# The head of a one-core kernel in written order: tokens loaded in pairs, other engines for copies and type tables, maxima in four row blocks, constants behind the scores

## The chip, the core and the metric

The kernel runs on one core of a Trainium2 chip. The core's engines each work through their own list of instructions: TensorE (PE; its weight loads are listed as PEld), VectorE (DVE), ScalarE (ACT), GpSimd (POOL) and SyncE (SP), which here only issues transfers. They wait for one another through semaphores. Data lies in device memory, in SBUF (128 partitions) or, for matmul results, in PSUM. The metric is the device time of one execution in microseconds (us); lower is better.

## What is computed

Two layers work on `x` of 8 sequences, 256 tokens, 128 features, all in float32. Only the first step of the first layer is touched by the change:

```python
attn_in = jnp.tanh(jnp.einsum('bsd,da->bsa', hidden, W1) + b1)     # A = 32
scores = jnp.einsum('bsa,a->bs', attn_in, v)
prefix_m = l <= j;  postfix_m = l >= j;  cloze_m = l != j
mask = where(pt == 0, prefix_m, where(pt == 1, postfix_m, cloze_m))  # pt: one type per sequence
p = softmax(where(mask, scores[:, None, :], NEG_INF), axis=-1)
pooled = einsum('bjl,bld->bjd', p, hidden) / cnt
...
logits = einsum('bld,ed->ble', pooled, gate_weight)
kth_val = sort(logits.reshape(-1))[expert_k - 1]
gates = logits * (logits >= kth_val)
h = gelu(einsum('bld,ehd->bleh', pooled, w1) + b1)                   # 8 experts, 512 hidden
x = x + sum over experts of gates * (h @ w2 + b2)
```

The second layer adapts each sequence by its language (two small matrices, a layer norm), takes the two best of eight experts for each token, runs those experts and adds the result to `x`.

## The kernel before

The work falls into three stages. The **head** (lines 90 to 345) loads `x`, scores the tokens and pools them. The **first layer** (`layer`, L801 and L781) runs all eight experts on all 2048 tokens, five units of 512 or 256 tokens; beside it generators (`poolings`, `threshold`, `adapt`) are advanced a step at a time by `pump`. The **second layer** fetches tiles of 128 sorted rows and runs one expert on each (L857, L866), then adds up and stores.

The head in the order of its data. There are four groups `g`, each of two sequences, so 512 tokens. `xg[g]` holds the tokens, two on each partition and sequence, in rows of `XW` = 137: 128 features, 8 gate products, and a one. SP and ACT each load half of every group (L105). TensorE turns the tokens (`xTp`, L227); the copy to `xT` goes to ScalarE for groups 0 and 2 (L232) and to VectorE for 1 and 3 (L230). `products` multiplies by `W1` and the gate columns (`xa`, L206), VectorE adds `b1` (L209), ScalarE takes the tanh (L210) and copies the gate products into `xg` (L211). `scores` multiplies by `v` and sums (L214, L215) into `sl`, one column for 128 tokens. `bv` holds `b1` and `v` on all partitions, made by a matmul of `diag` and `ones` (`bvp`, L234, L236).

The softmax needs for each query the largest score that it may see. `sl` is turned to rows, one per sequence (`scp`, L251), two scans run along them, forwards and backwards (L254, L256), and two operations make of them and of `out8` (what a sequence's type rules out) the maxima, 8 rows (L258, L259). A matmul with one column of `ident`, broadcast, copies a row to all 128 partitions: `tops` (L265). `probs` subtracts them from a table of masks, chosen by the sequence's type (`hide`, `kind`, L274), and ScalarE takes the exponential with the score as bias (L277). `pool` multiplies by the tokens (`poolp`, L287), `scaled` divides by the sum and by `cnt` (L294 to L298), and `turned` turns the result for the first layer (`poolTp`, L304; `poolT`, L306).

Small tables come from the types `ptb`: `e0`, `e1`, `kind`, `out8`, on VectorE (L135 to L152). GpSimd issues the loads of `col`, `bva` and `ptb`, builds `ident` and `hide`, and then the constants of later stages: `nhalf`, `rank`, `tri`, `dest`, `kth`, `empty`, `steps`, `nowhere`, `used` (L349 to L509). `used` is first read by a copy of eight columns on VectorE (L705), which belongs to the second layer's lists. `pass_time` (L193) is a filler: matmuls into a PSUM tile that nobody reads.

The order in each engine's list is set by a scheduler from the program, except where a block is marked as manual (`manual_schedule`), which keeps it as written. Before, only the end of the kernel is so marked.

Of the kernel before, what the change touches and what calls it, by code (L numbers as in the profile page):

```python
# [10 lines left out]
F32 = mybir.dt.float32  # L11
I32 = mybir.dt.int32
AF = mybir.ActivationFunctionType
# [58 lines left out]
def tile_adaln_ffn_d2(ctx: ExitStack, tc: tile.TileContext, x, ptype, lang, cols, b1v,  # L72
# [17 lines left out]
    xg = []  # L90
    for g in range(NG):

        xg.append(keep.tile([P, GT, XW], F32, tag="xg", name=f"xg{g}"))
    ptb = const.tile([P, B], I32, name="ptb")
# [3 lines left out]
    ident = const.tile([P, P], F32, name="ident")  # L98
    make_identity(nc, ident)
    nc.gpsimd.dma_start(out=col, in_=cols)  # L100
    nc.gpsimd.dma_start(out=bva, in_=b1v)
    nc.gpsimd.dma_start(out=ptb, in_=ptype.partition_broadcast(P))
    for g in range(NG):
        for i, queue in enumerate((nc.sync, nc.scalar)):
            queue.dma_start(out=xg[g][:, 2 * i:2 * i + 2, :D], in_=xv[g, i])  # L105
    nc.sync.dma_start(out=lgi, in_=lang.partition_broadcast(P))

# [12 lines left out]
    ones = const.tile([P, P], F32, name="ones")  # L120
    nc.vector.memset(ones, 1.0)
# [4 lines left out]
    for i, (sign, keeps) in enumerate(((-1, ALU.is_ge), (1, ALU.is_ge), (1, ALU.not_equal))):  # L126
        nc.gpsimd.affine_select(out=hide[:, i, :], in_=hide[:, i, :],
                                pattern=[[sign, 2], [-sign, 2], [-2 * sign, P]], compare_op=keeps, fill=NEG,
                                base=0, channel_multiplier=2 * sign)
    jrow = const.tile([P, 2], F32, name="jrow")  # L130
# [4 lines left out]
    nc.vector.tensor_copy(ptf, ptb)  # L135
    e0 = const.tile([P, B], F32, name="e0")
    nc.vector.tensor_scalar(e0, ptf, 0.0, None, ALU.is_equal)
    e1 = const.tile([P, B], F32, name="e1")
    nc.vector.tensor_scalar(e1, ptf, 1.0, None, ALU.is_equal)
    kind = const.tile([P, B], I32, name="kind")  # L140
    with nc.allow_low_precision("0, 1 or 2"):
        nc.vector.scalar_tensor_tensor(kind, e0, 2.0, e1, ALU.mult, ALU.add)
        nc.vector.tensor_scalar(kind, kind, -1, 2, ALU.mult, ALU.add)


    out8 = const.tile([B, 3], F32, name="out8")
    for i, flag in enumerate((e0, e1)):
        own = small.tile([B, B], F32, tag="own", name=f"own{i}", bufs=2)
        nc.vector.scalar_tensor_tensor(own, flag[:B, :], NEG, ident[:B, :B], ALU.mult, ALU.mult)
        nc.vector.tensor_reduce(out8[:, i:i + 1], own, AX.X, ALU.add)  # L150
    nc.vector.tensor_tensor(out8[:, 2:3], out8[:, 0:1], out8[:, 1:2], ALU.add)
    nc.vector.tensor_scalar(out8[:, 2:3], out8[:, 2:3], -1.0, NEG, ALU.mult, ALU.add)  # L152
# [30 lines left out]
    fwd, bwd, rows = fwd[:B, :], bwd[:B, :], top[:B, :]  # L183
    nc.gpsimd.memset(fwd[:, 0:1], NEG)
    nc.gpsimd.memset(bwd[:, S - 1:], NEG)
    nc.gpsimd.memset(top, 0.0)

# [7 lines left out]
    pass_time(5, ident, ident)  # L195


    sl = small.tile([P, NT], F32, tag="sl", name="sl", bufs=1)
    xas = {}

    def products(g):

        space = (psy, "y") if g < 2 else (psb, "big")
        xa = space[0].tile([P, GT, A + E], F32, tag=space[1], name=f"xa{g}")
        for t in range(GT):
            nc.tensor.matmul(xa[:, t, :], lhsT=xT[g][:, t * P:(t + 1) * P], rhs=col[:, C_W1:C_W1 + A + E],  # L206
                             start=True, stop=True)
        pass_time(1, ident, xT[g][:, :S])
        nc.vector.tensor_tensor(at[:, g], xa[:, :, :A], bv[:, 0].unsqueeze(1).to_broadcast([P, GT, A]), ALU.add)  # L209
        nc.scalar.activation(at[:, g], at[:, g], AF.Tanh)  # L210
        nc.scalar.copy(xg[g][:, :, D:D + E], xa[:, :, A:])  # L211

    def scores(g):
        nc.vector.tensor_tensor(at[:, g], at[:, g], bv[:, 1].unsqueeze(1).to_broadcast([P, GT, A]), ALU.mult)  # L214
        nc.vector.tensor_reduce(sl[:, g * GT:(g + 1) * GT], at[:, g], AX.X, ALU.add)  # L215
# [5 lines left out]
    bvp = psy.tile([P, 2, A], F32, tag="y", name="bvp")  # L221
    bv = const.tile([P, 2, A], F32, name="bv")

    for g in range(NG):
        tp = psb.tile([P, GT, P], F32, tag="big", name=f"xTp{g}")
        for t in range(GT):
            nc.tensor.transpose(tp[:, t, :], xg[g][:, t, :D], ident)  # L227
        xT[g] = keep.tile([P, GN], F32, tag="xT", name=f"xT{g}")
        if g % 2:
            nc.vector.tensor_copy(xT[g], tp.rearrange("p t d -> p (t d)"))  # L230
        else:
            nc.scalar.copy(xT[g], tp.rearrange("p t d -> p (t d)"))  # L232
        if not g:
            nc.tensor.matmul(bvp.rearrange("p c a -> p (c a)"), lhsT=ones[:A, :],  # L234
                             rhs=diag.rearrange("k c a -> k (c a)"), start=True, stop=True)
            nc.vector.tensor_copy(bv, bvp)  # L236
        else:
            products(g - 1)
        if g > 1:
            scores(g - 2)  # L240
    products(NG - 1)
    scores(NG - 2)
    scores(NG - 1)
    kinds = []
    for b in range(B):
        kinds.append(nc.values_load(kind[0:1, b:b + 1], engines=(DVE,), min_val=0, max_val=2,
                                    skip_runtime_bounds_check_because="2 - 2 e0 - e1, of flags"))

    sp = pss.tile([B, S], F32, tag="sm", name="scp")
    for u in range(2):  # L250
        nc.tensor.transpose(sp.rearrange("b (p u) -> b p u", u=2)[:, :, u],  # L251
                            sl.rearrange("p (b u) -> p b u", u=2)[:, :, u], ident)
    pass_time(5, sl[:, NT - 1:].to_broadcast([P, P]), xT[0][:, :S])
    nc.vector.tensor_tensor_scan(fwd[:, 1:], sp[:, :S - 1], out8[:, 1:2].to_broadcast([B, S - 1]), NEG,  # L254
                                 ALU.max, ALU.add)
    nc.vector.tensor_tensor_scan(bwd[:, S - 2::-1], sp[:, :0:-1], out8[:, 0:1].to_broadcast([B, S - 1]), NEG,  # L256
                                 ALU.max, ALU.add)
    nc.vector.scalar_tensor_tensor(fwd, sp, out8[:, 2:3], fwd, ALU.add, ALU.max)  # L258
    nc.vector.tensor_tensor(rows.rearrange("b (u p) -> b p u", u=2), fwd.rearrange("b (p u) -> b p u", u=2),  # L259
                            bwd.rearrange("b (p u) -> b p u", u=2), ALU.max)  # L260
    tops = []
    for g in range(NG):
        tp = psb.tile([P, 2, S], F32, tag="big", name=f"top{g}")
        for i in range(2):
            nc.tensor.matmul(tp[:, i, :], lhsT=ident[:, 2 * g + i:2 * g + i + 1].to_broadcast([P, P]), rhs=top,  # L265
                             start=True, stop=True)
        tops.append(tp)
# [3 lines left out]
    def probs(b):  # L271
        g, i = b // 2, b % 2
        m = scratch(f"probs{b}")
        nc.vector.tensor_tensor(m, hide[:, bass.ds(kinds[b], 1), :].rearrange("p k (t j) -> p (k t) j", t=2),  # L274
                                tops[g][:, i, :].unsqueeze(1).to_broadcast([P, 2, S]), ALU.subtract)
        for lt in range(2):
            nc.scalar.activation(m[:, lt, :], m[:, lt, :], AF.Exp, bias=sl[:, 2 * b + lt:2 * b + lt + 1])  # L277
# [71 lines left out]
    nc.gpsimd.memset(nhalf, -0.5)  # L349
# [46 lines left out]
    nc.gpsimd.memset(nowhere, float(NOWHERE))  # L396

# [108 lines left out]
    used = const.tile([P, E], F32, name="used")  # L506

    holding = const.tile([P, E], F32, name="holding")
    nc.gpsimd.memset(used, 0.0)  # L509
# [63 lines left out]
    def adapt(u, acc):  # L573
# [11 lines left out]
        ha = work.tile([A + 1, 2, S], F32, tag="ha", name=f"ha{u}")  # L585
        nc.gpsimd.memset(ha[A:A + 1, :, :], 1.0)  # L586
# [428 lines left out]
```

## Time and profile before

| what | value |
|---|---|
| five runs | 379.33, 382.74, 383.48, 385.68, 377.87 us |
| their median | 382.74 us |
| the profiled execution, its own time | 378.91 us |
| its span, first to last instruction | 377.1 us |
| granted TensorE clock, mean | 0.98 |
| DMA | 46.12 MB, mean 122 GB/s |
| GpSimd busy | 95.6 us, 25% of the span |

All durations are from that one profiled execution. In the profile's lists L12 is line 12 of the kernel; a group's line names the tile written and those read, their partitions and elements, and how many instructions there were; a float32 matmul shows as two instructions, a transpose as one. Busy shares of 40 equal slices are given in tenths. Idle time is put down to the event that ended it. A timeline merges neighbouring instructions of one kind into one line, with the time from the first's start to the last's end.

The waits of the first 35 us, the larger ones, in all and the longest single one:

```profile
engine line waited for: us in total, times, longest us
ACT probs L277 <- DVE probs L274: 5.4, 1, 5.4
ACT front L210 <- DVE front L209: 4.5, 4, 1.7
ACT xT L232 <- PE xTp L227: 3.8, 2, 2.6
...
DVE diag L219 <- DMA bva<-in_b1v_dram: 3.6, 1, 3.6
...
PE idle L193 <- POOL ident masks.py:199: 2.6, 1, 2.6
```

### The profile page before, as it was taken

The page shows a single profiled execution, that of the slowest core. Times are in us where ns is not written, and L with a number is a line of the kernel's source. Part 1 is how long each engine was busy: PE and PEld are TensorE (multiplying, and loading weights), DVE is VectorE, ACT ScalarE, POOL GpSimd, SP SyncE. Part 2 cuts the span into 40 slices and gives each one's busy share as a digit, 9 for nine tenths or more (in the row PEclk, how much of TensorE's full clock was granted, in tenths as well). Part 3 has the DMA queues.
Part 4 walks back from the last instruction along what each step waited for, and adds up shares of the span by engine and source line. Part 5 has one row for each costly group of instructions (what it writes and reads, how often), then busy time and mean ns, then how long its engine had stood idle before and what let it go on. Part 6 is the DMA issues. An engine that isn't in the chain of part 4 may idle for free. (4 is left out here: it accounts for less than half of the span.)

```text
span 377.1 us, 5944 instructions
## 1 busy us (share of the span) xinstructions
PE 347.6 (92%) x1596; PEld 234.9 (62%) x1596; DVE 199.5 (53%) x835; ACT 166.7 (44%) x387; POOL 95.6 (25%) x141
## 2 busy tenths in 40 slices
PE   6999999999999999999999999999979987899920
PEld 6796444444444445444544688878859886799920
DVE  4676556551334676654611465786575674234344
ACT  2265443454453224333353335435625745566730
POOL 8100000000000030452160012072043655534450
PEclk9999999999999999999999999999989999999985
DMA  7935999004224201111130001124642653567426
GB/s 208 374 75 149 365 379 364 8 0 113 91 64 132 56 30 56 56 49 35 37 83 22 28 20 45 36 79 134 181 122 84 167 173 94 164 190 195 150 91 196
DMA packets 34466, 46.12 MB, mean 122 GB/s; under 512 B 5444, under 2 KB 17622, under 8 KB 34432
## 3 DMA queue, kind: packets, MB, share of 16 engines
q1 hardware_dynamic: 29888, 39.98, 35.3%
q0 software_dynamic: 2304, 4.37, 3.4%
q10 hardware_dynamic: 2240, 1.38, 1.2%
q8 instruction: 14, 0.23, 0.2%
q14 instruction: 20, 0.16, 0.2%
HBM read 31.57 MB, written 14.39 MB: 122 GB/s over the span
## 5 line engine op out<-in xcount | busy, mean ns | idle before, releaser
L803 ACT ACTIVATE hT_first<-hp_first,col 128x512 f32<-128x512 f32 (+1 forms) x160 | 93.4, 601 | 101.4 <-PE hp_first L801 99.4
L801 PE MATMUL hp_first<-poolT,w 128*128 128x512 f32 (+1 forms) x320 | 120.6, 512 | 0.0
L781 PE MATMUL yp_first<-hT_first,w 128*128 128x512 f32 (+1 forms) x320 | 120.5, 511 | 0.0
L781 PEld LDWEIGHTS yp_first<-hT_first,w 128*128 128x128 f32 x320 | 58.9, 190 | 42.5 <-issue 38.6
L801 PEld LDWEIGHTS hp_first<-poolT,w 128*128 128x128 f32 x320 | 59.0, 190 | 42.2 <-issue 37.2
L688 POOL DMA_INDIRECT xs<-zr,pos x32 | 32.3, 1008 | 65.3 <-DVE pos L686 27.9
L859 ACT ACTIVATE hs<-hps,b 128x128 f32<-128x128 f32 x144 | 40.3, 368 | 17.2 <-PE hps L857 8.2
L872 POOL DMA_INDIRECT ys<-yt,xt x36 | 35.7, 991 | 43.4 <-ACT hs L859 26.6
L866 PE MATMUL yps<-w,hs 128*128 x288 | 40.1, 282 | 3.3 <-DVE yt L870 1.7
L857 PE MATMUL hps<-xc,wt 128*128 128x128 f32 x288 | 39.4, 279 | 1.7 <-issue 1.7
L866 PEld LDWEIGHTS yps<-w,hs 128*128 128x128 f32 x288 | 35.7, 193 | 5.3 <-ACT hs L859 2.5
L769 DVE SCALAR_TENSOR_TENSOR part_first<-yp_first,col,gbc_first 128x512 f32<-128x512 f32 (+1 forms) x28 | 17.2, 616 | 40.4 <-PE yp_first L781 40.2
L857 PEld LDWEIGHTS hps<-xc,wt 128*128 128x128 f32 x288 | 36.0, 195 | 2.4 <-issue 1.4
L871 ACT ACTIVATE yt<-yt,xt 128x128 f32<-128x128 f32 x36 | 14.6, 405 | 22.3 <-issue 10.6
L850 DVE COPY b<-col 128x4 f32 x36 | 7.1, 197 | 25.3 <-ACT hs L859 22.4
L771 DVE TENSOR_TENSOR acc_first<-acc_first,part_first 128x512 f32<-128x512 f32 (+1 forms) x35 | 20.1, 581 | 0.6
L410 POOL DMA_DIRECT2D gd_L<-gT_L x1 | 0.7, 653 | 75.3 <-DVE gT_L L408 75.3
L586 POOL MEMSET ha<- 1x512 f32 x5 | 2.6, 516 | 67.6 <-PE dp L595 67.4
L870 DVE TENSOR_TENSOR yt<-yps,b2all 128x128 f32<-128x128 f32 x36 | 10.6, 294 | 13.4 <-PE yps L866 7.6
L848 DVE TENSOR_SCALAR xc<-xtp,col 128x128 f32<-128x128 f32 x36 | 14.4, 402 | 3.7 <-PE xtp L846 2.4
L789 ACT ACTIVATE y_first<-yp_first,col 128x512 f32<-128x512 f32 x8 | 5.5, 687 | 24.2 <-PE yp_first L781 24.2
L424 DVE TENSOR_SCALAR_CACHE_REDUCE fl<-logit,tr 128x128 f32<-128x128 f32 x46 | 13.5, 343 | 0.6
(213 smaller groups left out, 316.0 us busy)
## 6 DMA issues: line engine op xcount, KB each, us to landing
wt<-in_w_dram SPq DMA_DIRECT2D x36, 256.0 KB
xs<-empty SPq DMA_DIRECT2D x1, 8580.0 KB
w<-in_w_dram SPq DMA_DIRECT2D x24, 256.0 KB
gbc_first<-gd_L SPq DMA_DIRECT2D x24, 256.0 KB
xt<-xs SPq DMA_DIRECT2D x36, 65.0 KB
gbc_first<-gd_L SPq DMA_DIRECT2D x16, 128.0 KB
yg<-ys SPq DMA_DIRECT2D x5, 256.0 KB
lgb<-in_lgb_dram SPq DMA_DIRECT2D x8, 128.0 KB
```

The costliest lines, as they stand in the source:

```text
L688: move = nc.gpsimd.indirect_dma_start(out=xs, out_offset=bass.IndirectOffsetOnAxis(ap=pos[:, t:t + 1], axis=0), in_=zr[s][:, t, :], in_off ...
L769: nc.vector.scalar_tensor_tensor(part, y, bias, gbc, ALU.add, ALU.mult)
L771: nc.vector.tensor_tensor(accs[u], accs[u], part, ALU.add)
L781: nc.tensor.matmul(yp, lhsT=w2s[e][:, c, :], rhs=hT[:, c, :], start=(c == 0), stop=(c == HC - 1))
L801: nc.tensor.matmul(hp, lhsT=w1s[e][:, c * P:(c + 1) * P], rhs=sources[g][:, o * P:o * P + n], start=True, stop=True)
L803: nc.scalar.activation(hT[:, c, :], hp, act, bias=col[:, cb1 + e * HC + c:cb1 + e * HC + c + 1])
L848: nc.vector.tensor_scalar(xc, tp, col[:, C_LG:C_LG + 1], col[:, C_LB:C_LB + 1], ALU.mult, ALU.add)
L857: nc.tensor.matmul(hp[:, c, :], lhsT=wt[:, c * P:(c + 1) * P], rhs=xc, start=True, stop=True)
L859: nc.scalar.activation(hT[:, c, :], hp[:, c, :], AF.Gelu, bias=b1[:, c:c + 1])
L866: nc.tensor.matmul(yp, lhsT=hT[:, c, :], rhs=w21[:, bass.ds(ek, 1), c * D:(c + 1) * D], start=(c == 0), stop=(c == HC - 1))
L871: nc.scalar.activation(yt, yt, AF.Copy, scale=xt[:, D + 1:D + 2])
L872: move = nc.gpsimd.indirect_dma_start(out=ys, out_offset=bass.IndirectOffsetOnAxis(ap=xt.bitcast(I32)[:, D:D + 1], axis=0), in_=yt, in_off ...
```

## The change

All lines of the head are put under a manual schedule for TensorE, VectorE, ScalarE and GpSimd (`beginning`), which ends after the constants. Within it:

- Each group's tokens are loaded twice: first into `xp`, a tile of four of the scratch ring, with the two tokens of a partition side by side, by SP and ACT; then, by SP alone and ahead of the weights, into `xg` as before. The transposes read `xp`, the pooling reads `xg`.
- `ident` is finished before GpSimd issues its loads, and `bva` is issued ahead of `col`. The first filler reads `ones` instead of `ident` and runs seven times; other fillers change in number and place.
- All four `xT` copies are ScalarE's. Transposes of groups 2 and 3 stand between the products of groups 0 to 2. The copies of the gate products come after the last tanh.
- `e0`, `e1`, `kind` are made on GpSimd. `sl` becomes 2 x 128 columns with a group's two sequences at columns 32 g and 32 g + 1, so that the turned scores, the scans and the maxima lie on 128 partitions, a group in each block of 32; `at_home` and `out8` follow that layout, and `out8` comes between the scores of groups 1 and 2.
- The `tops` matmuls read 32 rows each, first all four groups' first sequence, then their second.
- GpSimd's `nhalf`, and so all constants behind it, wait for the last score. `used` and two tiles `ha` (their row of ones was set anew in every `adapt` before) are set at the end of them.
- In the lists, VectorE's `c1` and `cnt` operations now follow the eight `probs`; they stood among earlier work before. The copy out of `used` (L705 before, L733 after) stands right ahead of the first `probs`.

The core of the diff:

```diff
+        xp.append(work.tile([P, 2, S], F32, tag="scr", name=f"xp{g}", bufs=NSCR))
...
+    beginning.enter_context(tc.manual_schedule(engines={PE, DVE, ACT, POOL}))
+    ones = const.tile([P, P], F32, name="ones")
+    nc.vector.memset(ones, 1.0)
     make_identity(nc, ident)
+    nc.gpsimd.dma_start(out=bva, in_=b1v)
     nc.gpsimd.dma_start(out=col, in_=cols)
-    nc.gpsimd.dma_start(out=bva, in_=b1v)
     nc.gpsimd.dma_start(out=ptb, in_=ptype.partition_broadcast(P))
     for g in range(NG):
         for i, queue in enumerate((nc.sync, nc.scalar)):
-            queue.dma_start(out=xg[g][:, 2 * i:2 * i + 2, :D], in_=xv[g, i])
+            queue.dma_start(out=xp[g][:, i, :], in_=xv[g, i].rearrange("p u d -> p (u d)"))
     nc.sync.dma_start(out=lgi, in_=lang.partition_broadcast(P))
+    for g in range(NG):
+        for i in range(2):
+            nc.sync.dma_start(out=xg[g][:, 2 * i:2 * i + 2, :D], in_=xv[g, i])
...
-    nc.vector.tensor_copy(ptf, ptb)
+    nc.gpsimd.tensor_copy(ptf, ptb)
...
-    nc.vector.tensor_scalar(e0, ptf, 0.0, None, ALU.is_equal)
+    nc.gpsimd.tensor_scalar(e0, ptf, 0.0, None, ALU.is_equal)
...
+    nc.gpsimd.tensor_scalar(ptf, e0, -2.0, 2.0, ALU.mult, ALU.add)
+    nc.gpsimd.tensor_tensor(ptf, ptf, e1, ALU.subtract)
+    nc.gpsimd.tensor_copy(kind, ptf)
...
-    pass_time(5, ident, ident)
+    pass_time(7, ones, ones)
...
+    turned_tokens(0)
+    pass_time(1, ones, ones)
+    turned_tokens(1)
+    nc.tensor.matmul(bvp.rearrange("p c a -> p (c a)"), lhsT=ones[:A, :],
+                     rhs=diag.rearrange("k c a -> k (c a)"), start=True, stop=True)
+    nc.vector.tensor_copy(bv, bvp)
+    products(0)
+    turned_tokens(2)
+    bent(0)
+    products(1)
+    turned_tokens(3)
+    scores(0)
+    bent(1)
+    products(2)
+    pass_time(1, ident, xT[2][:, :P])
+    scores(1)
+    bent(2)
+    out8 = const.tile([P, 3], F32, name="out8")
+    for i, flag in enumerate((e0, e1)):
+        own = small.tile([P, B], F32, tag="own", name=f"own{i}", bufs=2)
+        nc.vector.tensor_tensor(own, flag, at_home, ALU.mult)
+        nc.vector.tensor_reduce(out8[:, i:i + 1], own, AX.X, ALU.add)
...
+    products(3)
+    pass_time(2, ident, xT[3][:, :S])
+    scores(2)
+    bent(3)
+    scores(3)
+    for g in range(NG):
+        nc.scalar.copy(xg[g][:, :, D:D + E], xas[g][:, :, A:])
...
+    tops = [psb.tile([P, 2, S], F32, tag="big", name=f"top{g}") for g in range(NG)]
+    for i in range(2):
+        for g in range(NG):
+            quadrant = slice(g * A, (g + 1) * A)
+            nc.tensor.matmul(tops[g][:, i, :], lhsT=ident[quadrant, g * A + i:g * A + i + 1].to_broadcast([A, P]),
+                             rhs=top[quadrant, :], start=True, stop=True)
+    pass_time(2, ident, xT[0][:, :S])
...
-    nc.gpsimd.memset(nhalf, -0.5)
+    begin = nc.gpsimd.memset(nhalf, -0.5)
+    tc.add_manual_dep(begin.ins, scored[-1].ins.name, SYNC, reason="leaves the vector engine its port until then")
...
+    used = const.tile([P, E], F32, name="used")
+    nc.gpsimd.memset(used, 0.0)
+    has = [const.tile([A + 1, 2, S], F32, name=f"ha{i}") for i in range(2)]
+    for ha in has:
+        nc.gpsimd.memset(ha[A:A + 1, :, :], 1.0)
+    beginning.close()
...
-    nc.gpsimd.memset(used, 0.0)
...
-        ha = work.tile([A + 1, 2, S], F32, tag="ha", name=f"ha{u}")
-        nc.gpsimd.memset(ha[A:A + 1, :, :], 1.0)
+        ha = has[u % 2]
```

## The prediction

> **What bounds the kernel now.** I read the page's busy shares and slices first, then the timeline of each engine over the first 45 us, then the waits of that stretch, then the instruction lists of both programs.
>
> ```profile
> PE 347.6 (92%) x1596; PEld 234.9 (62%) x1596; DVE 199.5 (53%) x835; ACT 166.7 (44%) x387; POOL 95.6 (25%) x141
> ...
> PE   6999999999999999999999999999979987899920
> ```
>
> TensorE is busy 92% of the span, from the first slice to the tail. So the change, all of it ahead of the first expert matmul, can move the end only by moving that matmul (30.22 us) along TensorE's line; from there both programs issue the same TensorE work.
>
> ```profile
> 2.62 2.50 PE L193 MATMUL idle<-ident 128*128 128x128 f32 x10 [2.62 <-POOL ident masks.py:199]
> 4.91 1.06 PE L227 MATMUL xTp<-ident,xg 128*128 128x128 f32 x4
> 6.58 0.68 PE L234 MATMUL bvp<-diag,ones 32*128 32x64 f32 x2 [0.61 <-DVE diag L219]
> 7.20 2.82 PE L227 MATMUL xTp<-ident,xg 128*128 128x128 f32 x12
> 9.81 1.28 PE L206 MATMUL xa<-col,xT 128*128 128x40 f32 x8
> ...
> 16.48 0.39 PE L251 MATMUL scp<-ident,sl 128*8 128x128 f32 x2 [0.92 <-DVE sl L215]
> ...
> 19.39 3.69 PE L265 MATMUL top<-front,ident 128*128 128x256 f32 x16 [0.36 <-DVE front L259]
> 22.91 5.80 PE L287 MATMUL poolp<-xg,probs 128*128 128x137 f32 x48
> 28.55 0.60 PE L304 MATMUL poolTp<-ident,pooled 128*128 128x128 f32 x4
> ...
> 30.22 1.12 PE L801 MATMUL hp_first<-poolT,w 128*128 128x512 f32 x2
> ```
>
> Columns: start, length, engine, line, operation, and in brackets the idle time before and who ended it. Up to 16.48 the chain is transposes, products, scores; then 2.9 us of VectorE scans with filler on TensorE; then TensorE is full from 19.39.
>
> ```profile
> 9.27 0.20 DVE L236 COPY bv<-bvp 128x64 f32<-128x64 f32 x1
> ...
> 9.68 1.27 DVE L230 COPY xT<-xTp 128x512 f32<-128x512 f32 x2
> ...
> 16.14 0.29 DVE L215 TENSOR_REDUCE sl<-front 128x4 f32<-128x128 f32 x1
> ...
> 18.64 0.60 DVE L259 TENSOR_TENSOR front<-front 8x256 f32<-8x256 f32 x1
> ...
> 19.35 0.15 DVE L705 COPY at<-used 128x8 f32<-128x8 f32 x1
> ...
> 20.52 4.88 DVE L274 TENSOR_TENSOR probs<-hide,top 128x512 f32<-128x512 f32 x8 [0.83 <-PE top L265]
> ```
>
> VectorE's copy of xT1 waits at 9.68 behind the type tables, which wait for ptb until 7.43. The fifth line counts later: a copy out of `used`, hoisted to just ahead of the probs.
>
> Call R the end of the last score: 16.14 + 0.29 = 16.43. The first expert matmul is at R + 13.79.
>
> **Up to R.** Removed: the type tables and `out8` ahead of the xT copies on VectorE, both VectorE xT copies (now ScalarE, 0.59 each at L232), two of four 256-column fillers between products, and the start on `ident` (2.62): the filler now reads `ones`, written 0.92 to 1.09, so TensorE starts at about 1.2. Added: two fillers, one more among the transposes, a 0.2 us memset of `sl` in VectorE's idle time before 6.32. The order is now worked through by TensorE's pitches (weight loads: filler 2.21/10 = 0.22, transpose 2.42/12 = 0.20, products 1.37 the first, about 0.8 a group later):
> 7 fillers 1.2 + 14 x 0.22 = 4.3; xTp0 5.1; filler 5.55; xTp1 6.35; bvp 6.85; products 0, first of their kind, 7.95; xTp2 8.65 (0.7, between cold and warm transposes); products 1 9.45; xTp3 10.15; products 2 10.95; short filler 11.2; products 3 12.0.
> ScalarE's copies fit between. `bva` now goes ahead of `col` on POOL's queue: `bva` landed at 6.25, 3.2 us after its issue ended, `ptb` 3.75 after; `col` issued by about 3.0 lands by 6.2 to 6.8, just in time for 6.85; if 0.7 later, R moves by as much. VectorE has the last word: after add 2 (11.3) and score 1 (11.9) stand the six `out8` operations, each waiting for the one before, at 0.17 (L150 to L152) about 1.0: 12.9. Then add 3 and two scores: 15.10 to 16.43 took 1.33 before, so R = 14.2. **Gain 2.2**, between 1.5 (TensorE at the slow pace throughout, `col` late) and 3.2 (fast pace from the second transpose, short `out8`).
>
> Doubled x loads: 1 MB more on SP's queue, ahead of all 16 first-layer weights, the languages' loads, w21, b2 and the 8.6 MB `xs` fill. At 276 to 357 GB/s (DMA rates of 2 to 10 us) 2.9 to 3.8 us. Cover: the 16 weights were issued by 14.3 and the first is read at 30.22; the `xs` fill left at 38.54 and the next issue on that queue is at 88.72, the first scatter past 130. Without that cover it would cost its 3.8. Price 0. The paired loads move 1 KB runs instead of 512 B: the first transpose was not waiting for data, 0. The `ha` memsets (0.52 each) leave GpSimd's later work, where GpSimd is a quarter busy: 0.
>
> **From R on.** Scans over 128 partitions instead of 8 keep their length (255 elements a partition either way). Three things move.
>
> (1) The constants. GpSimd's `nhalf` now waits for the last score, and 21 operations queue behind it, in this order.
>
> ```profile
> 6.00 0.13 POOL L349 MEMSET nhalf<- 128x4 f32 x1
> ...
> 8.04 0.12 POOL L509 MEMSET used<- 128x8 f32 x1
> ...
> 8.80 0.24 POOL L387 CAST steps<-kth 128x3 int32<-128x3 f32 x1
> ...
> 10.22 1.26 POOL L392 TENSOR_SCALAR steps<-steps 128x3 int32<-128x3 int32 x4
> ```
>
> The last line holds four operations. `used` was the 15th and done at 8.16; now it is behind the `steps` chain too. Pitches: `nhalf` to `steps` memset 1.93, two waits for a memset ahead of its select 0.3, zr copy 0.15, cast 0.23, first product 0.25, the four 1.26, nowhere and used 0.25: 4.4, plus 0.2 for two hand-overs. So `used` lands at R + 4.6 to 4.7. VectorE's copy out of `used` (after: L733) still stands right ahead of the probs in its list, and the eight probs, their register loads and all that follows wait behind it. The scans end at R + 2.8 and the probs began at R + 4.09; now they begin at R + 4.8 plus the first register load, no longer hidden: 0.06 (free) to 0.71 (SP's gap between an lgb issue and the next lw at L164, 16.51 to 17.22), I take 0.4: **R + 5.2**. This wait replaces the one for the tops.
>
> Beside it VectorE's last max (two SBUF inputs) meets GpSimd's 0.54 us memset of `empty`. VectorE's 8-element cast at 7.43 took 0.76 and its compare 0.54 beside GpSimd, against 0.18 at L143: up to 0.6 more, hidden under R + 5.2, but added if the `used` chain slows too (bound 0 to 0.6; nearest is 0, as L143 also ran beside GpSimd). [...]
>
> (2) The tops: eight matmuls over 32 rows, four to a round, in place of eight over 128. No row shows two row blocks at once: between 8 x 0.46 = 3.7 (as L265) and 2 x 0.46 = 0.9. The first prob waits for its tile's second matmul, now the fifth: R + 2.96 + 0.3 to 2.5, at most R + 5.5. Two fillers (0.92) follow. poolp therefore starts at R + 6.6 (R + 5.2, plus 0.73 to the exp and about 0.65 for it and the hand-over) or R + 7.5; before R + 6.48. I take the short end, because a round has separate inputs, weights and PSUM tiles. [...]
>
> (3) `cnt` (eight operations, four with waits, 1.1) moves from ahead of the probs to behind them. VectorE: probs R + 5.2 to 10.1, cnt 11.2, the first two `scaled` 1.5 (25.32 to 26.64 took 1.3, interleaved): R + 12.7. poolp's six end at R + 12.4, so poolTp0 starts at R + 12.7, was R + 12.0 by its weight load; **0.7 given back** (0.3 if `used` is early, 1.3 if the tops run one by one, up to 1.9 with the collision). Behind it the other `scaled`, 4.5 of VectorE time (27.81 to 33.50, less the copy's 0.68 and a wait of 0.52), reach poolTp1 about 0.7 late as well, no more.
>
> **Sum.** 378.91 (span 377.1 and 1.8 around it) - 2.2 + 0.7 = 377.4. That profiled run is 3.8 under the median of the five, 382.74, so the forecast on the median is **381.2**.
>
> **Rivals.**
> *Faster.* `used` arrives before the tops and rounds overlap: probs at R + 4.1, VectorE ready for poolTp0 at R + 11.6, first expert matmul R + 13.3, 0.45 won instead of 0.7 lost. With R 3.2 earlier: 3.7, 379.1; with an out8 block under 0.8, past 3.8. For: TensorE's early start. Against: GpSimd's 4.4 us.
> *Slower.* TensorE's clock falls back. Its idle before poolp grows from 0 to about 1.8 us, after one of 1.2 before the scores' turn. The same shape took 421 ns (xTp) and 272 ns (poolTp), and the slow pace lasted from 2.62 to 9.8. If 7.2 us at 1.8 times the pitch return, 3.2 are lost: 381.2 + 3.2 = 384.4; after both gaps 387.6. It decides at gaps past 1.7: after an idle 1.72 at 326.43 eight matmuls took 1.21 instead of 1.06, no fallback. [...]
> *Not what it says.* `col` late and `out8` in the way hold R at 15.7: nothing won, 382.7.
>
> **Chances.** What a measurement here can tell from no change is about 1%, 3.8 us. Forecast 0.50 (within 1% but for 0.05 faster and 0.03 slower by measurement), faster 0.28 (0.23 over 1%, rest within), slower 0.14 (0.09 over 1%), nothing 0.08. Sums: faster 0.28, same 0.60, slower 0.12. Range: the fast rival 379.1 less about 1.7 for the spread of medians (five runs span 377.87 to 385.68), to the slow one's single gap: 377.4 to 384.4.
>
> **What would show it.** R near 14.2; `used` ended by GpSimd past R + 4.5 with VectorE idle ahead of L733, released by POOL; poolp matmuls still 280 ns; poolTp0 at R + 12.7; first expert matmul 1 to 2 us before 30.2. Wrong if VectorE waits for the tops instead, if xTp stays at 421 ns past 9 us, or if what is won at the first expert matmul is not found at the end.

## The result, and the profile after

The changed kernel takes 376.94 us, the median of 52 runs (374.26 to 380.46), beside 380.81 us for the kernel before in 94 runs (376.64 to 386.91). The ratio is 0.9942, with a 95% interval of 0.9925 to 0.9958: 2.2 us won, clear of no change, but less than the 1% that one takes for a difference here. (The medians are of all runs; the ratio leaves out those over 1.5% above their kernel's fastest, 36 of the 94 and 2 of the changed kernel's, so it is nearer to 1.) On the median that the forecast was made on, the ratio gives 382.74 x 0.9942 = 380.5; the forecast was 381.2, its range 377.4 to 384.4. The profiled execution took 377.3 us, its span 375.6 us; the sum had 377.4, and that this close a match is partly luck is shown further down. The busy shares and slices of the page are almost those of before:

```profile
PE 347.8 (93%) x1604; PEld 234.8 (63%) x1604; DVE 198.4 (53%) x829; ACT 168.4 (45%) x389; POOL 95.9 (26%) x145
...
PE   8889999999999999999999999999979987999920
```

TensorE does the same work, 347.8 us of it, and the whole difference is in where the first expert matmul stands.

TensorE's timeline in the head of the changed kernel; the columns are as in the prediction (start, length, engine, line, operation, idle time before it and its releaser):

```profile
1.13 3.35 PE L193 MATMUL idle<-ones 128*128 128x128 f32 x14 [1.13 <-DVE ones L104]
4.28 1.06 PE L230 MATMUL xTp<-ident,xp 128*128 128x128 f32 x4
...
7.04 1.08 PE L207 MATMUL xa<-col,xT 128*128 128x40 f32 x8
...
13.85 0.41 PE L271 MATMUL scp<-ident,sl 128*128 128x128 f32 x2 [1.09 <-DVE sl L217]
...
16.82 1.15 PE L286 MATMUL top<-front,ident 32*128 32x256 f32 x16 [0.41 <-DVE front L278]
...
20.37 6.02 PE L310 MATMUL poolp<-xg,probs 128*128 128x137 f32 x48 [1.34 <-POOL empty L545]
26.26 0.41 PE L327 MATMUL poolTp<-ident,pooled 128*128 128x128 f32 x2
...
28.20 1.02 PE L829 MATMUL hp_first<-poolT,w 128*128 128x512 f32 x2
```

TensorE starts at 1.13 instead of 2.62, begins the products at 7.04 instead of 9.81, and reaches the first expert matmul at 28.20 instead of 30.22. The tops are new in kind: 1.15 us for 16 records (a float32 matmul leaves two), where the kernel before needed 3.69. In front of `poolp` stands an idle time that was not there. The releaser named in that bracket, a GpSimd cast, is not what `poolp` reads; its operand `probs` comes from VectorE and ScalarE. VectorE's list shows why it is late:

```profile
13.41 0.29 DVE L217 TENSOR_REDUCE sl<-front 128x4 f32<-128x128 f32 x1
...
16.04 0.64 DVE L278 TENSOR_TENSOR front<-front 128x256 f32<-128x256 f32 x1
18.28 0.57 DVE L733 COPY at<-used 128x8 f32<-128x8 f32 x1 [1.61 <-POOL used L422]
19.04 4.87 DVE L297 TENSOR_TENSOR probs<-hide,top 128x512 f32<-128x512 f32 x8 [0.18 <-PE idle L193]
```

The last score ends at R = 13.41 + 0.29 = 13.70. The maxima are done at 16.68, and then VectorE idles 1.61 us for the eight columns of `used`, which the second layer wants. GpSimd, released by that same last score, gets to them late in its block, behind the `steps` chain:

```profile
13.76 0.10 POOL L372 MEMSET nhalf<- 128x4 f32 x1 [4.44 <-DVE sl L217]
...
16.91 1.27 POOL L416 TENSOR_SCALAR steps<-steps 128x3 int32<-128x3 int32 x4
...
18.15 0.10 POOL L422 MEMSET used<- 128x8 f32 x1
```

### The profile page after: what moved, and what is told of

Its sections match the earlier page's. It is cut to its first block, busy times and chain, and to the rows that moved or that the text cites. A ratio compares the mean times of both kernels' runs of the same rounds, so it can differ in the third digit from the quotient of the medians.

```text
span 375.6 us, 5975 instructions
## 1 busy us (share of the span) xinstructions
PE 347.8 (93%) x1604; PEld 234.8 (63%) x1604; DVE 198.4 (53%) x829; ACT 168.4 (45%) x389; POOL 95.9 (26%) x145
## 4 chain that ended last, share of the span: by engine, by line
PE 84%; DVE 6%; issue 3%; DMA 2%; POOL 2%; another core or an unknown queue 1%; DVEq 0%; SPq 0%; ACT 0%; POOLq 0%
PE hp_first L829 30%; PE yp_first L809 29%; PE yps L894 8%; PE hps L885 7%; PE dp L623 1%; DMA yg<-ys 1%; PE poolp L310 1%; PE adp L616 1%; PE idle L193 1%; PE xtp L874 1%; PE l1p L663 1%; PE xa L207 1%; PE xTp L230 1%; DVE yt L898 1%
## 5 line engine op out<-in xcount | busy, mean ns | idle before, releaser
L506 POOL TENSOR_TENSOR rstd_l<-ve_l,nhalf 128x4 f32<-128x4 f32 (+1 forms) x5 | 4.7, 936 | 72.4 <-DVE ve_l L504 72.3
```

## The experiments

A total of a single execution can't tell these kernels apart: the kernel before alone spans 376.64 to 386.91 us. So for single executions I read three marks in the head: R, the start of the first prob, and the start of the first expert matmul. Totals are compared only for the two kernels that were run twelve times each. The table's last column is when the trace's records of the granted TensorE clock begin, each time with the full clock; they fit the moments at which the matmuls become short. In two runs the clock later fell to 0.50 for a while, in the head still: from 16.48 to 19.89 in no_gate, from 11.05 to 17.87 in tables_copies_dve. Each row is one execution; after and again are the same program, and their R differ by 0.42.

| kernel | R | first prob | first expert matmul | full clock from |
|---|---|---|---|---|
| before | 16.43 | R + 4.09 | 30.22 = R + 13.79 | 10.42 |
| after | 13.70 | R + 5.34 | 28.20 = R + 14.50 | 6.86 |
| again | 13.28 | R + 5.35 | 27.78 = R + 14.50 | 5.91 |
| used_early | 13.46 | R + 4.25 | 26.87 = R + 13.41 | 4.47 |
| used_cnt | 13.47 | R + 4.65 | 26.79 = R + 13.32 | 6.29 |
| no_gate | 16.64 | R + 5.33 | 31.14 = R + 14.50 | 6.24 |
| no_gate_used | 13.20 | R + 4.22 | 26.58 = R + 13.38 | 4.49 |
| tops_128 | 13.75 | R + 5.55 | 28.46 = R + 14.71 | 6.95 |
| fill_3 | 17.07 | R + 5.38 | 31.62 = R + 14.55 | 20.32 |
| before_fill | 15.56 | R + 4.03 | 29.28 = R + 13.72 | 4.89 |
| tables_copies_dve | 14.47 | R + 5.45 | 29.10 = R + 14.63 | 4.22 |
| one_load | 12.86 | R + 5.33 | 27.36 = R + 14.50 | 4.80 |
| used_cnt_out8 | 12.93 | R + 4.65 | 26.25 = R + 13.32 | 4.97 |
| best_one_load | 13.33 | R + 4.65 | 26.64 = R + 13.31 | 7.11 |

**The wait for `used`.** First the suspected wait alone is taken away, by an earlier memset:

```diff
+    used = const.tile([P, E], F32, name="used")
+    nc.gpsimd.memset(used, 0.0)
     ptf = const.tile([P, B], F32, name="ptf")
...
     nc.gpsimd.memset(nowhere, float(NOWHERE))
-    used = const.tile([P, E], F32, name="used")
-    nc.gpsimd.memset(used, 0.0)
```

> Changed kernel with one memset moved: `used` is set ahead of the type tables instead of behind the constants; everything else stays gated behind the last score. Measured from the last score R = 13.70 of the changed kernel. Theory (the wait for `used` took 1.1 us of the gain): VectorE's copy out of it leaves the path, the first prob waits for the tops and starts near 17.9 instead of 19.04, and with VectorE's chain probs, cnt, scaled unchanged behind it the first expert matmul starts near 27.1 instead of 28.20. Rival 1 (TensorE's tops, fillers and poolp set it anyway): probs earlier, first expert matmul within 0.3 of 28.20. Rival 2 (the tops' first result is itself late): first prob at 18.7 or later.

VectorE's timeline of used_early:

```profile
15.80 0.63 DVE L280 TENSOR_TENSOR front<-front 128x256 f32<-128x256 f32 x1
17.71 4.87 DVE L299 TENSOR_TENSOR probs<-hide,top 128x512 f32<-128x512 f32 x8 [1.28 <-PE top L288]
```

Between the maxima and the probs only the tops are left to wait for. The copy out of `used` now runs at 6.76 and takes 0.16. The first prob comes 1.09 sooner behind R, and so does the first expert matmul. So this wait cost 1.1 us, measured by itself.

The second step also puts the eight `cnt` operations back ahead of the probs (the block at L338 to L341 moved above the loop over `probs(b)`).

> The kernel with `used` set early, and besides the eight operations for `cnt` ahead of the probs, in VectorE's wait for the tops. Theory (1.25 us of `cnt` behind the probs is the rest of what was given back): VectorE is ready for poolTp0 about 1.2 earlier than with `used` alone, so TensorE's poolp becomes the bound: poolTp0 right behind the sixth poolp, near 25.2, and the first expert matmul near 26.8, 0.3 to 0.4 ahead of `used` alone. Rival (poolp is the bound already there): no difference, within 0.1.

`poolTp0` now runs in one piece (25.30, 0.60 for four) instead of waiting 0.21 for its second half. But the probs start 0.4 later behind R, and the first expert matmul gains 0.09:

```profile
17.37 0.23 DVE L341 SCALAR_TENSOR_TENSOR cnt<-e,c,cnt 128x8 f32<-128x8 f32 x1
18.12 4.87 DVE L299 TENSOR_TENSOR probs<-hide,top 128x512 f32<-128x512 f32 x8 [0.52 <-POOL nowhere L422]
```

The 0.52 is put down to a GpSimd memset whose tile the probs don't read. What VectorE waited for there is open; the prediction's register loads, bounded there between 0.06 and 0.71, would fit. The theory's 0.3 to 0.4 did not come: with `used` early, the position of `cnt` is worth about 0.1, because what it saves behind the probs it costs in front of them.

Next the gate, the line that makes `nhalf` wait for the last score:

```diff
-    tc.add_manual_dep(begin.ins, scored[-1].ins.name, SYNC, reason="leaves the vector engine its port until then")
```

> Changed kernel without the dependence of `nhalf` on the last score: GpSimd builds its constants from about 9.3 on, beside VectorE's scores. Theory (the gate costs, as it makes `used` late; the two engines' sharing costs less): constants end before 14.5, probs start 4.1 to 4.3 behind the last score instead of 5.34; R itself moves from 13.70 to at most 14.3; first expert matmul between 27.1 and 27.7. Rival (the gate pays: GpSimd and VectorE hold each other up in the products by v, two operands in SBUF): single VectorE operations of 0.28 grow to 0.5 and more, R past 14.8, first expert matmul at 28.2 or later.

R came at 16.64, later than in the kernel before. The cause is neither of the two. Without the gate the copy out of `used` was put in among the scores, and there it found the same late memset. VectorE's and TensorE's timelines of no_gate:

```profile
13.57 0.57 DVE L732 COPY at<-used 128x8 f32<-128x8 f32 x1 [2.80 <-POOL used L421]
```

```profile
16.79 0.66 PE L271 MATMUL scp<-ident,sl 128*128 128x128 f32 x2 [4.29 <-DVE sl L217]
17.24 3.64 PE L193 MATMUL idle<-xT,sl 128*128 128x256 f32 x10
```

VectorE lost 2.80 us in the middle of its chain. TensorE idled 4.29, and behind that its fillers took 3.64 for ten, where they had taken 2.32; the granted clock was 0.50 there. They put the tops off to 20.81, so the R + 14.50 of the changed kernel came again, though the copy out of `used` was long done: the same number by another wait. So the gate was tested again with `used` early:

> GpSimd's second block no longer waits for the last score (as in no_gate), and `used` is zeroed ahead of the type tables, so that the copy out of `used` finds its operand early wherever it is put. Theory (no_gate lost its 2.9 us to that copy, placed among the scores, and to the idle TensorE behind it; GpSimd beside VectorE costs little): last score ends at 13.5 to 14.2, first expert matmul at 26.9 to 27.7, ahead of the changed kernel's 28.20. Rival (GpSimd's writes stretch VectorE's products, 0.49 against 0.28 us was seen once): last score at 14.3 to 16, first expert matmul at 27.8 or later.

The theory held, better than in its numbers: R 13.20, first expert matmul 26.58. VectorE's products run beside GpSimd's block (8.46 to 13.7) at 0.28 and 0.29 each, as they do with the gate:

```profile
12.59 0.28 DVE L218 TENSOR_TENSOR front<-front,bv 128x128 f32<-128x128 f32 x1
```

With `used` early, then, the gate is worth nothing that these executions show: R + 13.38 without it, R + 13.41 with it. The reason written into its line isn't borne out by them.

**The start, and TensorE's pace.** One kernel has three fillers in place of the first seven.

```diff
-    pass_time(7, ones, ones)
+    pass_time(3, ones, ones)
```

> Changed kernel with three fillers ahead of the first transpose instead of seven. Theory (the fillers end when data is there; next is the table `bv` from the load of bva at 5.9, and the products): first transpose at the landing of its tokens, 3.0 to 4.0 instead of 4.28, matmul by bv at most 0.4 earlier, R between 13.2 and 13.9. Rival 1 (the fillers hold the head up): R earlier by about 1.3. Rival 2 (they bring the fast pace sooner): transposes of 421 ns for longer than up to about 6.6, R later by 0.3 or more.

TensorE's timeline of fill_3:

```profile
3.68 1.08 PE L230 MATMUL xTp<-ident,xp 128*128 128x128 f32 x4 [0.90 <-POOL xg L128]
...
6.75 1.90 PE L207 MATMUL xa<-col,xT 128*128 128x40 f32 x8
...
13.93 1.77 PE L207 MATMUL xa<-col,xT 128*128 128x40 f32 x8
...
17.77 3.59 PE L193 MATMUL idle<-xT,sl 128*128 128x256 f32 x10
```

The transposes start 0.6 earlier and the products 0.3 earlier, and R is 3.4 later. Eight products take 1.77 to 1.90 instead of 0.98 to 1.08, and this lasts to the end of the head's scans at about 21 us, with hardly a gap in TensorE's work. The full clock was granted only at 20.32. So the second rival came, at ten times its size: the four fillers removed were worth 3.4 us in this execution. They keep the 0.90 gap out, but that the gap is the cause isn't shown; before_fill, below, has a longer one.

The reverse: the kernel before, with `ones` set first and eight fillers on `ones` in place of five on `ident`.

```diff
+    ones = const.tile([P, P], F32, name="ones")
+    nc.vector.memset(ones, 1.0)
     make_identity(nc, ident)
...
-    pass_time(5, ident, ident)
+    pass_time(8, ones, ones)
```

> The kernel before with one part of the change alone: `ones` set first, and 8 matmuls on `ones` in place of 5 on `ident` in front of the transposes, so that TensorE starts near 1.1 and has no gap before them. Theory (most of the head's gain is that TensorE's matmuls become short by 6.6 and not after 9): transposes of 4 still 421 ns each up to 6.6 at most and 275 after, last score at 14.5 to 15.7 against 16.43. Rival (the moves between the engines are the gain): last score within 0.4 of 16.43, whatever the matmuls' pace.

TensorE's timeline of before_fill:

```profile
1.14 3.79 PE L193 MATMUL idle<-ones 128*128 128x128 f32 x16 [1.14 <-DVE ones L100]
...
7.99 0.33 PE L227 MATMUL xTp<-ident,xg 128*128 128x128 f32 x1 [1.05 <-DMA xg<-in_x_dram]
...
8.61 1.08 PE L206 MATMUL xa<-col,xT 128*128 128x40 f32 x8
```

The products' first eight are short (1.08) at 8.61, where the kernel before had 1.28 at 9.81. R is 15.56, inside the theory's range, but the gain is 0.87 of the change's 2.73, with the full clock from 4.89 on instead of 10.42: a third, not most of it. Two things blur this. The scheduler also moved `bvp` behind the transposes and VectorE's first `xT` copy ahead of `diag`; and TensorE, now early, waited 1.05 for tokens.

The changed kernel once more, unedited:

> The changed kernel once more, nothing edited: how far the head moves between executions. Theory (when TensorE's matmuls become short varies between executions, 4.3 to 6.6 us were seen with almost the same head, and the products can't start before `col` lands at 6.8): last score at 12.9 to 13.9, copy out of `used` again waiting 1.3 to 2.5 us for GpSimd, first probabilities 5.2 to 5.5 behind the last score. Rival (the pace sets in at a fixed place in the program): matmuls short from 6.6 on again, last score within 0.1 of 13.70.

R moved by 0.42 (13.28 against 13.70), and behind R nothing moved: the copy out of `used` waited 1.60, the probs came at R + 5.35. The second four transposes took 0.78 where they had taken 1.06, and the products began at 6.64 instead of 7.04. So `col` can land by 6.6; the expectation's 6.8 was too late for it.

**The engines' share and the loads.** The type tables go back to VectorE (behind `diag`), and so do the `xT` copies of groups 1 and 3:

```diff
-    nc.gpsimd.tensor_copy(ptf, ptb)
+    nc.vector.tensor_copy(ptf, ptb)
...
-        nc.scalar.copy(xT[g], tp.rearrange("p t d -> p (t d)"))
+        if g % 2:
+            nc.vector.tensor_copy(xT[g], tp.rearrange("p t d -> p (t d)"))
+        else:
+            nc.scalar.copy(xT[g], tp.rearrange("p t d -> p (t d)"))
```

> Changed kernel with two parts undone: the six operations of the type tables and the xT copies of groups 1 and 3 are VectorE's again, in the place they had, behind `diag`. Theory (VectorE's wait for ptb at 7.4 to 7.6 and the tables hold up bv and xT1, which was the bound of the head before): bv at 9.3 or later instead of 7.15, R between 14.9 and 15.6, first expert matmul between 29.4 and 30.1, so over half of the head's gain gone. Rival (the order of the transposes and the early start of TensorE give the gain): R within 0.5 of 13.70.

R is 14.47, 0.77 later than in the profiled run and 1.19 later than in again, between the ranges of the theory (from 14.9) and of the rival (to 14.2). Here are the lines of TensorE that say how:

```profile
8.69 1.09 PE L195 MATMUL xa<-col,xT 128*128 128x40 f32 x8 [0.89 <-DVE xT L233]
...
12.89 2.05 PE L181 MATMUL idle<-xT,ident 128*128 128x256 f32 x4
```

VectorE's copy of `xT` stands behind the tables, TensorE waits 0.89 for it, and from about 11.1 on its matmuls are long again (four fillers 2.05 instead of 1.11), while the clock is granted at 0.50. How much of the 0.77 is VectorE's queue and how much the pace, this execution doesn't separate.

One kernel loads the tokens once, by SP and ACT, straight into `xg`, as before the change:

```diff
-            queue.dma_start(out=xp[g][:, i, :], in_=xv[g, i].rearrange("p u d -> p (u d)"))
+            queue.dma_start(out=xg[g][:, 2 * i:2 * i + 2, :D], in_=xv[g, i])
     nc.sync.dma_start(out=lgi, in_=lang.partition_broadcast(P))
-    for g in range(NG):
-        for i in range(2):
-            nc.sync.dma_start(out=xg[g][:, 2 * i:2 * i + 2, :D], in_=xv[g, i])
...
-            nc.tensor.transpose(tp[:, t, :], xp[g][:, t // 2, t % 2 * P:(t % 2 + 1) * P], ident)
+            nc.tensor.transpose(tp[:, t, :], xg[g][:, t, :D], ident)
```

> Changed kernel with one load of the tokens: straight into `xg`, in runs of 512 B, transposes from there; no second load. Theory (the head waits for TensorE's order, not for data): first transpose at 4.3 as now, R within 0.4 of 13.70, first expert matmul within 0.4 of 28.20. Rival (the paired load is where the gain of R comes from): transposes idle until DMA, R later by 1 us or more.

R came at 12.86, 0.84 earlier, which neither had. Two things had changed at once: `bva` landed at about 4.4 instead of 5.3 to 5.9, and the short matmuls set in earlier in this execution (full clock from 4.80 instead of 6.86). One kernel brings the gains together with the tokens loaded twice: `used` early, `cnt` ahead of the probs, and `out8` moved up into VectorE's gap behind the first products.

> `used` set early, `cnt` ahead of the probs, and the six operations of out8 moved from between the scores of groups 1 and 2 to VectorE's idle time between the sums of groups 0 and 1 (8.45 to 9.45). Theory: the sum of group 3 then starts when its products end, about 11.9 instead of 12.38, R near 13.3, first expert matmul near 26.4, 1.8 ahead of the changed kernel, 3.8 ahead of the kernel before; ratio to the kernel before about 0.990, to be told from 0.994 only if the runs spread little. Rival (e0 and e1 come from GpSimd too late for that gap, 8.2 and 8.4): the sum of group 1 starts past 9.5 and R stays at 13.7.

It took 374.84 us against 378.37, a ratio of 0.9902 (0.986 to 0.9943), with the first expert matmul at 26.25, 1.95 ahead of the changed kernel's. The interval overlaps that of the changed kernel, so as totals the two aren't told apart. The same with the tokens loaded once:

> `used` and cnt early and out8 in the gap behind the first products, as in used_cnt_out8, and the tokens loaded once, straight into the tile that the pooling reads. Theory (the second load of the tokens and the 128-token pairs cost the head 0.4 to 0.8 us, since `bva` and `col` land earlier without them): last score at 12.0 to 12.8, first expert matmul at 25.4 to 26.1, ratio to the kernel before 0.985 to 0.989. Rival (the loads are hidden, and the 0.84 that one_load gained came from TensorE's earlier short matmuls): last score at 12.9 to 13.5, first expert matmul at 26.2 to 26.8, ratio 0.989 to 0.992.

It took 364.61 us against 368.54 on its chip, a ratio of 0.9934 (0.989 to 0.9977). R is 13.33 and the first expert matmul at 26.64, both in the rival's ranges; the ratio itself tells neither apart. In this execution the short matmuls came late (`bvp` still took 0.66 at 6.60). The single load may save something where they come early: with the tokens loaded twice, TensorE then waited for `diag` and `col` together 0.76 us in used_early, 0.51 in used_cnt_out8 and 0.49 in no_gate_used; in one_load it waited for neither, and R was 12.86 there against 13.46 and 13.20 in used_early and no_gate_used, with the full clock about as early. At the median no gain of the single load is shown.

**The tops.** One kernel reads 128 rows in each, so that the eight run one behind the other.

```diff
-            nc.tensor.matmul(tops[g][:, i, :], lhsT=ident[quadrant, g * A + i:g * A + i + 1].to_broadcast([A, P]),
-                             rhs=top[quadrant, :], start=True, stop=True)
+            nc.tensor.matmul(tops[g][:, i, :], lhsT=ident[:, g * A + i:g * A + i + 1].to_broadcast([P, P]),
+                             rhs=top, start=True, stop=True)
```

> Changed kernel with the eight tops matmuls over all 128 rows as before, same order, same tiles. Theory (the four row blocks of a round run at once, 8 matmuls in 1.15 us): now 8 x 0.46 = 3.7, tops 16.8 to 20.5, fillers to 21.4, first poolp at 21.4 instead of 20.37, first prob near 19.4 instead of 19.04, first expert matmul near 29.0, 0.8 later. Rival (the short matmuls come from their 32 rows, not from running together, or the tops are hidden behind the wait for `used`): first expert matmul within 0.2 of 28.20.

TensorE's timeline of tops_128:

```profile
16.87 3.69 PE L286 MATMUL top<-front,ident 128*128 128x256 f32 x16 [0.40 <-DVE front L278]
...
21.26 5.79 PE L310 MATMUL poolp<-xg,probs 128*128 128x137 f32 x48
```

The tops take 3.69 again, and `poolp` starts 0.9 later, but without gaps; VectorE's chain sets `poolTp0`, and the first expert matmul is only 0.2 later behind R. So most of what the four row blocks save lies under VectorE's chain, which waits for `used`; what they are worth with `used` early was not run. The rival that 32 rows make the matmuls short in themselves isn't borne out: a single record is no shorter over 32 rows than over 128, 398 ns in the mean against 384 (the number behind the busy time; the profile models these ends), so it is by overlapping more that 16 of them fit into 1.15 us. The changed kernel, then tops_128:

```profile
L286 PE MATMUL top<-front,ident 32*128 32x256 f32 x16 | 1.1, 398 | 0.4 <-DVE front L278 0.4
```

```profile
L286 PE MATMUL top<-front,ident 128*128 128x256 f32 x16 | 3.7, 384 | 0.4 <-DVE front L278 0.4
```

## Why the forecast held, step by step

**R = 14.2, measured 13.70, and 13.28 in again.** The mechanism was right, the last term 0.5 too large. TensorE followed the list of starts closely: first products ended 8.12 (7.95 in the sum), third transposes 8.60 (8.65), second products 9.41 (9.45), third 10.69 (10.95). The mis-sized term is the stretch from these third products to `out8`: with the products 0.26 sooner, score 1 ended at 11.55 and not at 11.9. The six `out8` operations started 0.1 before its end and took the forecast's 1.0 (11.46 to 12.46, not 12.9), and R followed at 12.46 + 1.24, where the sum had 1.33. Where in the list the matmuls become short is luck as far as these runs tell: the full clock came at 6.86 here and at 5.91 in again.

**The wait that takes the place of the tops.** `used` R + 4.6 to 4.7: measured 18.25 = R + 4.55. The scans kept their length: 0.69 and 0.66 over 128 partitions, 0.68 and 0.65 over 8 before. First prob R + 5.2: measured R + 5.34, by other terms: the copy out of `used` took 0.57, not 0.15 as before, and behind it came 0.18, not 0.4. `poolp` R + 6.6: measured 20.37 = R + 6.67. This was the forecast's centre, and used_early shows it as a cause: 1.09 us.

**The tops overlap.** The short end was taken, and it held: 1.15 against 3.69, 3.2 times faster. Before the result no run showed two row blocks at once: the short end, 2 x 0.46 = 0.9, was the author's estimate. The trace of after shows 1.15 for the two rounds of four.

**0.7 given back.** `poolTp0` at R + 12.7 came at 26.26 = R + 12.56, its second half at R + 13.18, and the first expert matmul moved from R + 13.79 to R + 14.50: the 0.7. The chain is the forecast's too: behind the probs VectorE works through `cnt` to 25.10, then through two `scaled`, and the second half of `poolTp0` waits for their end at 26.82. VectorE's rows and TensorE's of the changed kernel, and TensorE's of used_cnt:

```profile
24.87 0.23 DVE L341 SCALAR_TENSOR_TENSOR cnt<-e,c,cnt 128x8 f32<-128x8 f32 x1
...
26.40 0.42 DVE L320 TENSOR_TENSOR pooled<-poolp,rs 128x256 f32<-128x256 f32 x1
```

```profile
26.88 0.44 PE L327 MATMUL poolTp<-ident,pooled 128*128 128x128 f32 x2 [0.21 <-DVE pooled L320]
```

```profile
19.45 6.02 PE L312 MATMUL poolp<-xg,probs 128*128 128x137 f32 x48 [0.65 <-POOL empty L544]
25.30 0.60 PE L329 MATMUL poolTp<-ident,pooled 128*128 128x128 f32 x4
...
26.79 1.02 PE L828 MATMUL hp_first<-poolT,w 128*128 128x512 f32 x2
```

What failed is the 0.3 that the prediction kept of it if `used` came early. used_early turned it into a gain of 0.38 (R + 13.41), which the rival's R + 13.3 for an early `used` had better, and moving `cnt` then added 0.09. `cnt` early with the wait still there was not run. It would fit into VectorE's 1.61 us of idling; if `poolTp0` then stood 5.85 behind the start of `poolp` and the first expert matmul 1.49 behind that, as in used_cnt, the first expert matmul would come at R + 14.0. By this estimate `cnt`'s place is worth 0.5 of the 0.7 as long as the wait lasts: the two overlap, and taking away the wait alone is enough.

**The doubled loads at 0.** The covers named did hold: the first-layer weights started only at 9.88 (4.44 before), the `xs` fill left at 42.24 (38.54), and the next issue on that queue came at 86.59. What the prediction passed over is that `bva` and `col` may land later beside the doubled loads: TensorE waited 0.5 to 0.8 us for them in three executions with early short matmuls, and not at all in the profiled one. `diag`, which needs `bva`, started at 4.2 and 4.4 in the two kernels with a single load and at 5.3 to 5.9 in the others of the changed kernel.

**GpSimd beside VectorE, 0 to 0.6, hidden.** The max took 0.64 (0.60 before), so the 0.6 did not come there, nor the prediction's "up to 1.9 with the collision"; that this max and GpSimd hold each other up isn't shown. What took longer beside it was GpSimd's cast to `steps`: 0.44 at 16.17, against 0.19 at 10.87 in no_gate_used, so some 0.25 of `used`'s lateness; by what, isn't shown.

**The slower rival** was met in size, by another way, and bounded wrong. Long matmuls cost 3.4 us of R in fill_3 against the 3.2 of the rival, but there the clock did not fall back; it was granted in full only at 20.32. It did fall back in no_gate, behind an idle time of 4.29, and in tables_copies_dve, where the longest idle time since TensorE's start was 0.89. So "It decides at gaps past 1.7" fell; and no slow pace followed 1.05 in before_fill, nor 1.09 and 1.34 in the changed kernel. What decides is open. It is not the gap's length alone.

**From the head to the end.** 2.02 us won at the first expert matmul are 1.5 in the span and 2.2 in the ratio. At the end of the first layer they are still there: the last group of eight second matmuls began at 252.62 before and begins at 250.49, 2.13 sooner. What differs in the end comes past 260 us, where the granted clock was 0.98 before and 0.96 after in the two profiled runs. So the sum's 377.4 was met at 377.3 by misses that cancel: the head won 2.02 instead of 1.5, and 0.5 was lost again behind it.

Of the 2.73 us of R, then, the early start gave 0.87 by itself, and the moves off VectorE gave 0.77 or more, part of it through the pace. The remainder, with the new order of transposes between products in it, was not run alone. Each of these figures is from one execution, and R is early or late with the clock. Where the full clock came at 4.5 to 4.9, R was 15.56 with the early start alone (before_fill) and 13.46 and 13.20 in the changed kernel with `used` early; so at a like pace all that is not the early start is worth some 2.1 to 2.4.

## What to carry to other kernels

When a block of constants is put behind a wait, look up the first reader of every one of them in each engine's list, not in the program's text: here the reader of an eight-column tile of the second layer stood ahead of the first layer's critical operations, and one memset put back in front is worth half as much as the whole change won. Early fillers ahead of the first real matmul can be worth more than the gap that they close: with four fewer, in one execution here, a gap of 0.90 stood ahead of the transposes and R came 3.4 us later, though that the gap is the cause isn't shown. And judge changes in a head by marks in the head: single totals here scatter more than the change is worth.

## What the runs showed of the hardware

**When TensorE's matmuls become short varies, with the same program.** With seven fillers from 1.13, the first four transposes took 1.06 us in the profiled run and in again, but 0.71 in no_gate_used and 0.60 in tables_copies_dve, whose TensorE lists are the same up to there; the second four took 1.06, 0.78, 0.60 and 0.60. The trace's clock records say when the full clock came in these four: at 6.86, 5.91, 4.49 and 4.22. The views of the profile read 1.00 ahead of the first record too, so there the pace shows in the durations alone. A later fall does show, as in tables_copies_dve (window, its length, TensorE's busy time and matmuls, granted clock, DMA share, GB/s):

```profile
9.00:11.00 2.00, 2.00 (x20) 1.00 0.65 187
11.00:13.00 2.00, 2.00 (x12) 0.51 0.85 287
```

The changes lie whole multiples of 3.41 us apart: 6.24, 16.48 and 19.89 in no_gate; 4.22, 11.05 and 17.87 in tables_copies_dve. Why these multiples, and what sets the moment, isn't shown. In no_gate the clock fell in an idle time of 4.29, in tables_copies_dve with no idle time longer than 0.89 since TensorE's start. And in fill_3 the full clock came only after some 17 us of nearly gapless work.

**`diag` took longer beside GpSimd's selects.** `diag`, 32 x 64 from two SBUF inputs, took 0.21 at 5.90 in the changed kernel, behind the selects. When `bva` came early it took 1.15 and 1.30, and ended within 0.1 of GpSimd's selects on `hide`. VectorE's line in one_load and in best_one_load, and GpSimd's in best_one_load:

```profile
4.37 1.15 DVE L218 TENSOR_TENSOR diag<-ident,bva 32x64 f32<-32x64 f32 x1 [1.40 <-DMA bva<-in_b1v_dram]
```

```profile
4.21 1.30 DVE L220 TENSOR_TENSOR diag<-ident,bva 32x64 f32<-32x64 f32 x1 [1.24 <-DMA bva<-in_b1v_dram]
```

```profile
3.54 1.89 POOL L130 TENSOR_SCALAR_AFFINE_SELECT hide<-hide 128x512 f32<-128x512 f32 x3
```

The ends are 5.52, 5.51 and 5.43, although the starts differ. So in these two executions the earlier `bva` brought no end of `diag` before 5.5. That the selects hold it until then would fit these rows; no run takes them away. The copy out of `used` took 0.57 at 18.28 beside the `ha` memsets and 0.16 at 6.76 in used_early; by what, no run here shows.

**The same program differs in the second layer.** The changed kernel took 377.3 us in its profiled run and 364.72 in again, on chip 2. The kernel before is faster on that chip as well: a median of 368.54 us in 18 runs, against 378.37 in 17 on chip 8. The same two stretches in both (window, its length, TensorE's busy time and matmuls, granted clock, DMA share, GB/s), after first, then again:

```profile
130.00:260.00 130.00, 129.68 (x459) 1.00 0.18 48
260.00:340.00 80.00, 73.07 (x537) 0.96 0.55 151
```

```profile
130.00:260.00 130.00, 129.72 (x461) 1.00 0.17 49
260.00:340.00 80.00, 76.95 (x616) 1.00 0.62 169
```

Up to 260 us they agree; behind it one execution has the full clock and gets 15% more matmuls done in the same time. The clock's 4% alone isn't that much; what else differs isn't shown.
